# A chain of four convolution layers: how layer 2 takes its first images, gives its last ones to layer 3, and where layer 3's first matrices are loaded

## The chip, the cores and the metric

The kernel runs on one core of a Trainium2 chip. The metric is the device time of one execution in microseconds (us), lower being better; the time of before is the median of three runs. Besides them one execution was profiled, and all starts, waits and durations below are from that one.

## The reference

Four layers, each `x = x + conv_i(groupnorm(x))`, on 32 images of 96 channels and 56 x 56 points, all in fp32 at the edges. `groupnorm` has 32 groups of three channels, so that its mean and variance need every point of three channels of one image.

```python
x = x + _L0_conv_ref(_gn(x), ...)   # 1x1 to 576, 3x3 depthwise, squeeze-excite, 1x1 to 96
x = x + _L1_conv_ref(_gn(x), ...)   # 3-level Haar wavelet, 5x5 depthwise at each level
x = x + _L2_conv_ref(_gn(x), ...)   # 1x1 to 576, 3x3 depthwise, 1x1 to 96, 4-bit quantised
x = x + _L3_conv_ref(_gn(x), L3_conv_diff_metric)   # 9x9 depthwise, kernels from 2x2 metrics
```

## The kernel before

**Layers and intermediates.** Layers 0 and 2 go image by image (channels on partitions); layers 1 and 3 go channel by channel (rows of the image on partitions, all 32 images in the free dimension), layer 1 in 48 pairs of channels. Between the layers x lies in DRAM as `y0`, `y1` and `y2`, each in six tensors of 16 channels (`GR`). In DRAM the 32 images of a point stand side by side, so that one image's piece of a row is 14 floats, 56 B, and that of two images is 112 B. A channel-wise layer can begin only when the last image of the layer before it is stored; an image-wise layer only when the last channel is.

**Who issues transfers, and in which order.** All DMAs are issued by SP, in order, on eight semaphores that I call lanes: a DMA waits until the one eight places before it has landed. In layers 1 and 3 SP's order is written by hand (`MANUAL_SP`, around lines 990 and 1471); in layers 0 and 2 the order of PE, DVE and ACT is (`MANUAL`), and a scheduler puts SP's instructions where it finds them due.

**Layer 1** (lines 785 to 1021). At each step the loads for a pair three ahead are issued; `level1` (939 to 961) makes channel c's result `y` (line 949, three buffers) and stores it to `y1` (958). The matmuls are at lines 892 to 936, the normalisation of x by `nr` is on DVE at 867 and 868. Layer 1's first loads are `X<-y` (735, 738), after the last stores of layer 0, which are left over as `LastStores` (203 to 212) and issued in layer 1.

**From layer 1 to layer 2.** `Layer2` (1024 to 1133) holds two image buffers `pairs`: `kept` (images 0 and 1) and `xt1` (images 2 and 3). While layer 1 runs, `begin` (1117) loads them from `y1` by groups of 16 channels as these are finished, up to group 4. Of the last group, `nearly` (1124) loads 14 channels, 80 to 93, just before channel 94 is finished, in two DMAs of 343 KB; channels 94 and 95 go `straight` (1129) from `y` in SBUF into the buffers, four DMAs of 12 KB each, and also into `y1`. `xt1` first serves as the place where layer 2's weights are quantised. Layer 2 starts with the statistics of image 0 (line 102), then group norms (1202 to 1219) and the quantised activations (1241, 1255), then its first matmuls (1277).

**Layer 2** (1137 to 1376). `add` (1342) finishes a tile of an image, a quarter of its rows; `store` (1354) comes after an image's four. Images are stored by pairs when the second is done (line 225: six DMAs, one a group, 3584 pieces of 112 B). The last two differ: image 30 is stored whole by itself when it is done (six DMAs of 3584 pieces of 56 B); image 31 is stored by tiles as they are finished (`store_tile`, 196, line 200: six DMAs a tile, 896 pieces of 56 B, 49 KB), tiles 0 and 1 in layer 2 and tiles 2 and 3 as `LastStores` in layer 3. Images 30 and 31 both lie in `kept`.

**Layer 3** (1428 to 1507). For each channel: `images` loads X (735, 738, three DMAs), `matrices` loads its banded matrices `raw` (763 to 765: one DMA of 128 partitions, two of 16; 215 KB in all), ACT arranges them as `T` (747), DVE normalises (1460, 1461), 12 matmuls (1468), DVE adds X (1469), and the result is stored (1506). Loads run four channels ahead; every eighth channel the norms of eight channels come in one DMA. The first two left stores are issued between the matrices of channels 0 and 1, two more after channel 1's images, and then one every six channels.

Of the kernel before, what the change touches and what calls it, by code (L numbers as in the profile page):

```python
# [10 lines left out]
F32 = mybir.dt.float32  # L11
# [9 lines left out]
B, C, H, W = 32, 96, 56, 56  # L21
# [10 lines left out]
PH = HH * NPH  # L32
# [3 lines left out]
GR = 16  # L36
# [152 lines left out]
def groups(t, y, at, store=False, of=range(C // GR)):  # L189

    for g in of:
        part = t[g * GR : (g + 1) * GR], at(y[g])
        yield part[::-1] if store else part


def store_tile(nc, y, xt, i, g):

    rows = slice(i * 2 * RT * NPH, (i + 1) * 2 * RT * NPH)
    for to, of in groups(xt[:, rows], y, lambda y: y[:, rows, B - 1, :], store=True, of=[g]):
        nc.sync.dma_start(to, of)  # L200


# [12 lines left out]
def store_images(nc, y, im):  # L215

    b = im["b"]
    if b == B - 2:
        t, at = im["xt"], b
    elif b % 2 and b < B - 1:  # L220
        t, at = im["pair"], slice(b - 1, b + 1)
    else:
        return
    for to, of in groups(t, y, lambda y: y[:, :, at, :], store=True):
        nc.sync.dma_start(to, of)
# [402 lines left out]
NK = 3  # L628
# [128 lines left out]
LOW = 96  # L757


def load_matrices(nc, pool, t, c):  # L760

    raw = pool.tile([128, 2, NK * PH], F32, tag="raw", name="raw")
    nc.sync.dma_start(raw[:, 0], t[c, :128])
    nc.sync.dma_start(raw[LOW:PH, 1], t[c, LOW:PH])
    nc.sync.dma_start(raw[PH:, 1], t[c, 128:])
    return raw
# [18 lines left out]
def layer1(ctx, tc, w, y0, left, made, norm, t1, t2, t3, y1, k2, behind):  # L785
# [4 lines left out]
    nc = tc.nc  # L790
# [148 lines left out]
    def level1(st, j, h):  # L939
        if h == 0:  # L940
            st["y"] = io.tile([PH, 2, B, W4], F32, tag="y", name="y", bufs=3)
        if st["i"]:
            st["pf"][j, h] = pfine.tile([128, W4, B], F32, tag="f", name="pc1")
            coarse(st, j, h, True)
            fine(st, j, h, False)
        else:
            coarse(st, j, h, False)
        ps = st["pf"][j, h]
        nc.vector.scalar_tensor_tensor(
            st["y"][:, h], ps[:PH].rearrange("p q b -> p b q"), st["nr"][j][:PH, 2 * B : 2 * B + 1], st["X"][j][:PH, h],  # L950
            ALU.add, ALU.add)
        if h == 1:
            c = 2 * st["i"] + j
            if c == C - 2:
                k2.nearly()
            if c >= C - 2:
                k2.straight(c, st["y"], 0)
            nc.sync.dma_start(y1[c // GR][c % GR].rearrange("(h p) b q -> p h (b q)", h=2),
                              st["y"].rearrange("p h b q -> p h (b q)"))
            if c >= C - 2:  # L960
                k2.straight(c, st["y"], 1)

    def begin(st):
# [16 lines left out]
    sts = {}  # L980
# [43 lines left out]
class Layer2:  # L1024
# [96 lines left out]
                self.nc.sync.dma_start(pair[g * GR : (g + 1) * GR], self.y1[g][:, :, 2 * i : 2 * i + 2, :])  # L1121
            self.begun = g + 1

    def nearly(self):

        for i, pair in enumerate(self.pairs):
            self.nc.sync.dma_start(pair[C - GR : C - 2], self.y1[-1][: GR - 2, :, 2 * i : 2 * i + 2, :])

    def straight(self, c, y, i):

        for h in range(2):
# [2 lines left out]


@with_exitstack
def layer2(ctx, tc, S, k2, y1, y2):

# [201 lines left out]
    def add(im, i):  # L1342
        for j in range(2):
            n = 2 * i + j
            v = im["xt"][:, 2 * n * 2 * RT : 2 * (n + 1) * 2 * RT, :]
            nc.vector.scalar_tensor_tensor(
                v, im["ps"][i][:C, j, :NT].rearrange("c (r q) -> c r q", q=W4), s3, v, ALU.mult, ALU.add)
        if im["b"] == B - 1:
            tile_stats(nc, parts, im["xt"], i)
            if i < 2:  # L1350
                for g in range(C // GR):
                    store_tile(nc, y2, im["xt"], i, g)

    def store(im):
        b = im["b"]
        if b == B - 1:
            nc.vector.bn_aggr(mv_all[:, B - 1, :], parts.rearrange("c a b -> c (a b)"))
            norm.last(bank(name="pl"))
            return
        channel_stats(nc, sm, im["xt"], mv_all[:, b, :], "t")  # L1360
        store_images(nc, y2, im)
        if b % 2:
            fetch(b + 5)
        if b == B - 2:
            norm.begin()
        del ims[b]
# [6 lines left out]
    with tc.manual_schedule(engines=MANUAL):  # L1373
        others = [t for t in L2_ORDER.split() if t[0] not in "ano" and "+" not in t]
        run_steps(step, image, L2_ORDER, other={-1: L2_FIRST, B - 1: " ".join(others) + L2_LAST, B: "", B + 1: ""})
    return LastStores(nc, y2, k2.pairs[0][:C, :, 1, :], (2, 3)), norm


def diffusion_kernels(tc, cp, w, behind):
# [45 lines left out]


@with_exitstack
def layer3(ctx, tc, w, y2, left, made, norm, td, out):


    nc = tc.nc
    cp = ctx.enter_context(tc.tile_pool(name="l3c", bufs=1, reuse_waits="tile"))
    io = ctx.enter_context(tc.tile_pool(name="l3i", bufs=6, reuse_waits="tile"))
    psum = ctx.enter_context(tc.tile_pool(name="l3p", bufs=8, space=PSUM, reuse_waits="tile"))
    sts = {}

    AHEAD, NN = 4, 8
    norms = {}

    def load_norms(c):  # L1440

        if c % NN == 0:
            norms[c] = io.tile([128, NN, 2 * B + 1], F32, tag="nr", name="nr", bufs=3)
            rows = norm[c : c + NN].rearrange("c x -> (c x)").unsqueeze(0)
            nc.sync.dma_start(norms[c].rearrange("p c x -> p (c x)"), rows.to_broadcast([128, NN * (2 * B + 1)]))

    def matrices(c):
        sts.setdefault(c, {})["raw"] = load_matrices(nc, io, td, c)

    def images(c):  # L1450
        X = sts.setdefault(c, {})["X"] = io.tile([128, 2, B, W4], F32, tag="X", name="X")
        load_halves(nc, X, y2[c // GR][c % GR])

    def normal(st, h):

        if h == 0:
            st["x"] = io.tile([128, 2, B, W4], F32, tag="x", name="x")
        scale, bias = (st["nr"][:, i * B : (i + 1) * B].unsqueeze(2).to_broadcast([128, B, W4]) for i in range(2))
        v = st["x"][:, h]
        nc.vector.tensor_tensor(v, st["X"][:, h], scale, ALU.mult)  # L1460
        nc.vector.tensor_tensor(v, v, bias, ALU.add)  # L1461

    def filtered(st, h):
        if h == 0:
            st["y"] = io.tile([PH, 2, B, W4], F32, tag="y", name="y")
        ps = psum.tile([PH, B, W4], F32, tag="c", name="pc")
        for n, (k, to, of) in enumerate(shifts(W4, NK)):
            nc.tensor.matmul(ps[:, :, to], st["T"][:, h, k, :], st["x"][:, h, :, of], start=(n == 0), stop=(n == NK - 1))  # L1468
        nc.vector.tensor_tensor(st["y"][:, h], ps, st["X"][:PH, h], ALU.add)

    with tc.manual_schedule(engines=MANUAL_SP):
        pick = cp.tile([C, 2, 128], F32, tag="pick", name="pick")
        nc.sync.dma_start(pick, w["pick"])
        matrices(0)
        left.issue(2)
        matrices(1)
        for c in range(2):
            images(c)
        made.store(norm)
        left.issue(2)  # L1480
        images(2)
        load_norms(0)
        matrices(2)
        images(3)
        matrices(3)
        both = cp.tile([128, 2, 2 * B + 1], F32, tag="nr0", name="nr0")
        for c in range(-2, C):
            if 0 <= c < C - AHEAD:
                load_norms(c + AHEAD)
                images(c + AHEAD)  # L1490
                matrices(c + AHEAD)
            if c % 6 == 4:
                left.issue(1)
            cur, far = sts.pop(c, None), sts.get(c + 2)
            if far:
                far["nr"] = norms[(c + 2) // NN * NN][:, (c + 2) % NN] if c >= 0 else both[:, c + 2]
                far["T"] = arranged(nc, io, far["raw"])
                if c == -2:
                    made.spread(both, pick, psum.tile([128, 2, 2 * B + 1], F32, tag="c", name="pr0"))
            for h in range(2):  # L1500
                if far:
                    normal(far, h)
                if cur:
                    filtered(cur, h)
            if cur:
                nc.sync.dma_start(out[c].rearrange("(h p) b q -> p h (b q)", h=2),
                                  cur["y"].rearrange("p h b q -> p h (b q)"))


def kernel_body(tc, w, x, out):  # L1510
    nc = tc.nc
    with ExitStack() as ctx:
# [37 lines left out]
        with ExitStack() as ctx2:  # L1550
            k2 = Layer2(ctx2, tc, S, w, y1, kept, row)

            def behind(pair):
                k2.prepare(pair)
                if not k2.stages:
                    k2.begin(min(2 * pair, C - GR))

            layer1(tc, w, y0, left, made, norm1, t1, t2, t3, y1, k2, behind)
            left, made = layer2(tc, S, k2, y1, y2)
        layer3(tc, w, y2, left, made, norm3, td, out)  # L1560

# [140 lines left out]
```

## Time and profile before

| | |
|---|---|
| runs | 5734.16, 5743.59, 5745.54 us; median 5743.59 |
| the profiled execution | 5735.72 us, of which its span 5733.9 |
| PE, DVE, ACT busy | 96%, 82%, 73% of the span |
| chain of waits, shares | PE 83%, DMA 6%, ACT 4%, DVE 3% |
| last y0 stores land; first matmul of layer 1 | 2667.24; 2674.43 |
| last y of layer 1 (end); first matmul of layer 2 (1277) | 3565.10; 3588.93 |
| last add of layer 2, tile 3 (end); first matmul of layer 3 | 5268.57; 5298.42 |
| layer 3: start of the last matmul | 5728.83 |

Starts are counted from the span's beginning. A lane's landing is the last of a DMA's records. The chain of waits goes back from the last instruction, each step being what released the next; where it lists a DMA, PE and the rest stood waiting for that transfer. The timeline of SP shows when it issued, so a long row of SP is mostly waiting for a lane or for data, not moving bytes.

### The profile page before, as it was taken

What the parts mean: (1) busy time and instruction counts of PE and PEld (TensorE: products, weight loads), DVE (VectorE), ACT (ScalarE), POOL (GpSimd) and SP (SyncE); (2) the same over time, 40 slices, a digit from 0 to 9 for tenths busy, and PEclk for the clock granted to TensorE, in tenths of its full rate; (3) what the DMA queues carried; (4) which work ended last, traced back from release to release, by engine and by line L of the source; (5) the groups of instructions that cost most, each with busy time, mean ns of one, the idle gap of its engine ahead of it and who ended that gap; (6) DMA issues with size and microseconds to landing.
All of it is one profiled execution on the core that took longest, in us unless ns stands there. A gap on an engine that the chain in (4) does not pass through costs nothing.

```text
span 5733.9 us, 137279 instructions
## 1 busy us (share of the span) xinstructions
PE 5498.2 (96%) x59704; PEld 3067.5 (53%) x59704; DVE 4693.9 (82%) x5413; ACT 4173.6 (73%) x6024; POOL 240.2 (4%) x158
## 2 busy tenths in 40 slices
PE   5999999999999999997999998999999999997999
PEld 2333333343333333333566665777788777775444
DVE  6999999999999999996776665767777777774777
ACT  5888888888888888884566554777777777774555
POOL 5000000000000000000000000000000000000000
PEclk9999999999999999997999999999999999998999
DMA  3123333332222332214576667478687796857888
GB/s 99 16 56 61 61 58 58 57 59 48 49 54 56 61 59 53 53 18 73 143 151 148 148 148 111 20 52 48 42 54 44 52 53 41 53 30 46 240 248 247
DMA packets 1306473, 454.45 MB, mean 79 GB/s; under 512 B 1123710, under 2 KB 1301814, under 8 KB 1303950
## 3 DMA queue, kind: packets, MB, share of 16 engines
q1 hardware_dynamic: 1305869, 445.67, 51.5%
q8 instruction: 468, 7.67, 0.6%
q14 instruction: 136, 1.11, 0.1%
HBM read 284.47 MB, written 214.08 MB: 87 GB/s over the span
## 4 chain that ended last, share of the span: by engine, by line
PE 83%; DMA 6%; ACT 4%; DVE 3%; issue 2%; POOL 1%; SPq 1%; ACTq 0%; DVEq 0%; POOLq 0%
PE psd L492 18%; PE psd L1296 13%; PE psj L547 10%; PE ps L425 8%; PE pc L930 7%; PE ps L1277 7%; PE pse L448 6%; PE psj L1339 3%; DMA X<-y 3%; PE pc L1468 2%; PE pc L918 2%; PE pa L892 2%; ACT hi L1247 2%; PE pc L908 1%; ACT u L1267 1%
## 5 line engine op out<-in xcount | busy, mean ns | idle before, releaser
L466 DVE SCALAR_TENSOR_TENSOR h<-hpad,l_wdw,h 128x3136 f32<-128x3136 f32 x512 | 1782.0, 3481 | 9.1
L492 PE MATMUL psd<-plane,filt 128*32 128x392 f32 (+5 forms) x16384 | 1083.3, 485 | 0.0
L1296 PE MATMUL psd<-apad,diag 64*64 64x392 bf16 x20736 | 917.1, 330 | 62.8 <-issue 59.0
L1296 PEld LDWEIGHTS <-diag 64*64 64x64 bf16 x20736 | 689.1, 106 | 285.9 <-issue 111.2
L492 PEld LDWEIGHTS psd<-plane,filt 128*32 128x32 f32 (+1 forms) x16384 | 389.4, 108 | 675.0 <-issue 622.1
L1267 ACT ACTIVATE u<-ps,o,s 128x784 int16<-128x784 f32 x576 | 536.5, 1002 | 164.1 <-PE ps L1277 145.1
L747 ACT COPY T<-raw 32x112 f32<-32x112 f32 (+2 forms) x1440 | 462.9, 384 | 254.8 <-DMA raw<-tdiff 217.4
L1267 ACT ACTIVATE a<-psd,o,s 128x784 int16<-128x784 f32 x448 | 423.7, 998 | 273.3 <-PE psd L1296 273.2
L425 PE MATMUL ps<-xn,l_wboth 96*128 96x392 f32 (+1 forms) x1536 | 465.9, 505 | 23.7 <-ACT xn L407 22.9
L466 DVE SCALAR_TENSOR_TENSOR hc<-hhalf,l_wdw,hc 128x1568 f32<-128x1568 f32 x256 | 473.7, 1850 | 16.2 <-ACT hc L459 9.5
L1277 PE MATMUL ps<-hi,l_w1q 96*128 96x392 f32 x1280 | 463.0, 362 | 6.7 <-DVE u L1265 3.8
L930 PE MATMUL pc<-x,T 128*112 128x416 f32 (+1 forms) x1152 | 446.6, 524 | 3.4 <-DVE x L868 3.4
L1277 PE MATMUL ps<-lo,l_w1q 96*128 96x392 f32 x1280 | 438.2, 342 | 2.9 <-DVE lo L1255 2.9
L1468 PE MATMUL pc<-x,T 128*112 128x416 f32 (+1 forms) x1152 | 420.7, 526 | 18.3 <-DVE x L1461 10.3
L448 PE MATMUL pse<-xn,l_wboth 96*32 96x392 f32 x4096 | 392.3, 501 | 4.5 <-ACT hab L469 4.5
L425 PEld LDWEIGHTS ps<-xn,l_wboth 96*128 96x128 f32 (+1 forms) x1536 | 219.4, 173 | 248.9 <-issue 53.8
L1468 PEld LDWEIGHTS pc<-x,T 128*112 128x112 f32 x1152 | 203.9, 178 | 234.7 <-issue 196.3
L469 ACT ACTIVATE hab<-psd,o,s 128x784 f32<-128x784 f32 x256 | 283.8, 1113 | 59.5 <-PE psd L492 57.5
L435 ACT ACTIVATE hpad<-ps,o,s 128x784 f32<-128x784 f32 x256 | 278.0, 1102 | 50.5 <-PE ps L425 49.0
L547 PE MATMUL psj<-h,wg 128*32 128x392 f32 x3072 | 306.8, 514 | 0.2 <-DVE wg L534 0.2
L547 PE MATMUL psj<-hab,wg 128*32 128x392 f32 x3072 | 305.2, 510 | 0.0
L452 ACT ACTIVATE plane<-pse,o,s 128x784 f32<-128x784 f32 x256 | 255.7, 999 | 26.2 <-PE pse L448 21.6
(265 smaller groups left out, 7622.9 us busy)
## 6 DMA issues: line engine op xcount, KB each, us to landing
X<-y SPq DMA_DIRECT2D x192, 392.0 KB
y<-xt SPq DMA_DIRECT2D x108, 392.0 KB
y<-y SPq DMA_DIRECT2D x96, 392.0 KB
out_dram<-y SPq DMA_DIRECT2D x96, 392.0 KB
twav<-zwav SPq DMA_DIRECT2D x768, 36.8 KB
y<-kept SPq DMA_DIRECT2D x72, 392.0 KB
xt<-y SPq DMA_DIRECT2D x59, 392.0 KB
xt<-in_x_dram SPq DMA_DIRECT2D x8, 2352.0 KB
```

The costliest lines, as they stand in the source:

```text
L425: nc.tensor.matmul(ps[p, j, :NT], wexp[:, k * 128 : k * 128 + 128][:, m], im["xn"][:, j, rows, :].rearrange("c h w -> c (h w)"), start=Tru ...
L448: nc.tensor.matmul(ps[f * GC : (f + 1) * GC, half, :NT].rearrange("p (r w) -> p r w", w=W2), wexp[:, c : c + GC], im["xn"][:, f % 2, r0 : ...
L466: nc.vector.scalar_tensor_tensor(h2, taken(im, k, t), wdw[:, k, t : t + 1], h2, ALU.mult, ALU.add)
L469: nc.scalar.activation(view, ps, AF.Silu, bias=bi[1][:, c : c + 1], scale=sc[1][:, c : c + 1], accum_out=accum)
L492: nc.tensor.matmul(ps[at * GC : (at + 1) * GC, r, :NT].rearrange("p (r w) -> p r w", w=W2)[:, r0 - half * n : r1 - half * n, q0:q1], filt[ ...
L547: nc.tensor.matmul(ps[s * GC : (s + 1) * GC, t, :NT].rearrange("c (m r q) -> c r q m", m=2, q=W4), wg[p, k, c * GC : (c + 1) * GC], phases ...
L747: nc.scalar.copy(to.rearrange("x t (p s) -> x t p s", p=NPH), v[:, k])
L930: nc.tensor.matmul(ps[:PH, to], st["T"][j][:, h, k, :], st["x"][:, j, h, of], start=first and n == 0, stop=not first and n == NK - 1)
L1267: nc.scalar.activation(out, ps, AF.Identity, bias=o[:, c : c + 1], scale=s[:, c : c + 1])
L1277: nc.tensor.matmul(ps[:, j, :NT], w1[:, k * 128 : k * 128 + 128], im[part][:, r0 : r0 + RT, :].rearrange("c h w -> c (h w)"), start=(part ...
L1296: nc.tensor.matmul(ps[q, j, :NT].rearrange("p (r w) -> p r w", w=W), diag[p, k, t, :], v, start=(t == 0), stop=(t == 8))
L1468: nc.tensor.matmul(ps[:, :, to], st["T"][:, h, k, :], st["x"][:, h, :, of], start=(n == 0), stop=(n == NK - 1))
```

## The change

Three parts, which don't depend on each other but share code.

- **Image 30 is stored with image 31.** `store_images` is called only up to image 29. `store_tile` takes both images of `kept`: the same 24 DMAs (12 in layer 2, 12 left for layer 3), each now 896 pieces of 112 B, 98 KB. The six DMAs of image 30 are gone.
- **Matrices of layer 3 are loaded into `xt1`.** When image 28 is finished, `ahead` issues the loads of the matrices of the first nine channels (27 DMAs) into `xt1`, which holds no image by then; nine are as many as fit. Layer 3 uses them in place of its own for c < 9. Layer 3 now runs while layer 2's constants are still allocated.
- **Channels 80 to 95 go straight.** `nearly` is gone; each of the last 16 channels of layer 1 issues two DMAs to `kept`, its store to `y1`, and two DMAs to `xt1`: 64 straight DMAs instead of 8 and the two big loads.

```diff
@@ store_tile
-    for to, of in groups(xt[:, rows], y, lambda y: y[:, rows, B - 1, :], store=True, of=[g]):
+    at = B - 1 if len(xt.shape) == 3 else slice(B - 2, B)
+    for to, of in groups(xt[:, rows], y, lambda y: y[:, rows, at, :], store=True, of=[g]):
@@ load_matrices
-def load_matrices(nc, pool, t, c):
-    raw = pool.tile([128, 2, NK * PH], F32, tag="raw", name="raw")
+def load_matrices(nc, pool, t, c, raw=None):
+    if raw is None:
+        raw = pool.tile([128, 2, NK * PH], F32, tag="raw", name="raw")
@@ layer1, level1
-            if c == C - 2:
-                k2.nearly()
-            if c >= C - 2:
+            if c >= C - GR:
                 k2.straight(c, st["y"], 0)
...
-            if c >= C - 2:
+            if c >= C - GR:
                 k2.straight(c, st["y"], 1)
@@ Layer2
-    def nearly(self):
-        for i, pair in enumerate(self.pairs):
-            self.nc.sync.dma_start(pair[C - GR : C - 2], self.y1[-1][: GR - 2, :, 2 * i : 2 * i + 2, :])
@@ layer2, add
-                    store_tile(nc, y2, im["xt"], i, g)
+                    store_tile(nc, y2, im["pair"], i, g)
@@ layer2, store
-        store_images(nc, y2, im)
+        if b == B - 4:
+            ahead()
+        if b < B - 2:
+            store_images(nc, y2, im)
@@ layer2
-    return LastStores(nc, y2, k2.pairs[0][:C, :, 1, :], (2, 3)), norm
+    return LastStores(nc, y2, k2.pairs[0][:C], (2, 3)), norm
@@ layer3
-        sts.setdefault(c, {})["raw"] = load_matrices(nc, io, td, c)
+        sts.setdefault(c, {})["raw"] = raws[c] if c < len(raws) else load_matrices(nc, io, td, c)
@@ kernel_body
-            left, made = layer2(tc, S, k2, y1, y2)
-        layer3(tc, w, y2, left, made, norm3, td, out)
+            n = 2 * NK * PH
+            room = k2.pairs[1].rearrange("p r i q -> p (r i q)")
+            raws = [room[:, c * n : (c + 1) * n].rearrange("p (a b) -> p a b", a=2) for c in range(room.shape[-1] // n)]
+            def ahead():
+                for c, raw in enumerate(raws):
+                    load_matrices(nc, None, td, c, raw)
+            left, made = layer2(tc, S, k2, y1, y2, ahead)
+            layer3(tc, w, y2, left, made, raws, norm3, td, out)
```

More of the change, by code (lines that the diff above doesn't have):

```diff
@@ L1136, in layer2 @@
 @with_exitstack
-def layer2(ctx, tc, S, k2, y1, y2):
+def layer2(ctx, tc, S, k2, y1, y2, ahead):
     nc = tc.nc
@@ L1427, in layer3 @@
 @with_exitstack
-def layer3(ctx, tc, w, y2, left, made, norm, td, out):
+def layer3(ctx, tc, w, y2, left, made, raws, norm, td, out):
     nc = tc.nc
```

## The prediction

> **What bounds the kernel now.** I read the page first: PE is busy 96% of the span, so time can only be won where PE stands still, or lost where it is made to.
>
> ```profile
> PE 5498.2 (96%) x59704; PEld 3067.5 (53%) x59704; DVE 4693.9 (82%) x5413; ACT 4173.6 (73%) x6024; POOL 240.2 (4%) x158
> ```
>
> The edits touch the seam of layers 0 and 1, layer 1's last eight pairs, the seams of layers 1 and 2 and of layers 2 and 3, and layer 3. The windows of these stretches (columns: stretch, length, busy PE, PEld, DVE, ACT, POOL, granted clock, DMA share, GB/s) show PE nearly empty at two seams, full in layer 1's end and short of full in layer 3:
>
> ```profile
> 3565.00:3589.00 24.00, 0.99 (x5) 0.86 (x5) 5.36 (x18) 1.88 (x2) 2.83 (x15) 0.60 1.36 82
> 3415.00:3565.00 150.00, 149.30 (x576) 90.15 (x576) 89.82 (x134) 75.77 (x204) 0.15 (x1) 1.00 0.61 119
> 5267.00:5299.00 32.00, 2.63 (x10) 2.17 (x10) 5.85 (x18) 5.01 (x15) 0.54 (x1) 0.54 1.01 65
> 5300.00:5733.00 433.00, 419.14 (x1151) 203.12 (x1149) 330.02 (x572) 225.82 (x658) 0.00 (x0) 0.99 0.86 244
> ```
>
> The chain of waits (start, length, what) at the seam of layers 1 and 2: last matmul, y, and then only DMA until layer 2's statistics at line 102.
>
> ```profile
> 3564.41 0.69 DVE y L949
> 3565.10 4.47 SPq L1133
> 3569.62 7.46 DMA kept<-y
> 3577.09 2.64 DMA xt<-y
> ...
> 3579.95 3.85 DVE sth L102 x8
> ```
>
> SP's timeline there says why: two big loads (L1127) stand ahead of the straight copies, and the first straight waits for its turn among eight DMA lanes.
>
> ```profile
> 3558.63 0.88 SPq L1127 DMA_DIRECT2D kept<-y  x1
> 3559.57 3.12 SPq L1127 DMA_DIRECT2D xt<-y  x1
> 3562.73 7.48 SPq L1133 DMA_DIRECT2D kept<-y  x2
> ```
>
> The seam of layers 2 and 3 in the chain, then on SP: the six stores of image 30 hold SP from 5227 to 5256, the twelve tile stores to 5281, and layer 3's first image read (L735) comes only at 5293.
>
> ```profile
> 5276.42 10.68 DMA y<-kept
> 5287.16 5.86 DMA y<-kept
> 5293.44 0.70 SPq L738
> ```
>
> ```profile
> 5227.19 29.21 SPq L225 DMA_DIRECT2D y<-kept  x6
> 5256.50 24.86 SPq L200 DMA_DIRECT2D y<-kept  x12
> ...
> 5285.58 1.90 SPq L200 DMA_DIRECT2D y<-kept  x2
> ...
> 5293.08 0.32 SPq L735 DMA_DIRECT2D X<-y  x1
> ```
>
> **What the Trainium skill says.** "DMA: Bandwidth & Descriptors", Why small descriptors are slow: every packet pays a fixed overhead besides its bytes. The trace agrees: the pair stores (3584 descriptors of 112 B) land 5.9 to 6.9 us apart, mean 6.3, or 1.76 ns a descriptor; image 30's (3584 of 56 B) 5.5 to 8.2, mean 6.8. Half the bytes saved nothing. The same page, Anatomy of one DMA, gives some 2.0 us fixed (written for DMAs issued by GpSimd); SP's smallest straights land 2.1 us or more after issue, so I use 2.1. "TensorE: Matmul & The Clock Gate", What's actually happening: an idle PE falls to half clock. It did at both seams (from 3569.63 to 3607.18 and 5269.47 to 5303.60); both gaps stay long enough to halve it, so I count no gain from the clock.
>
> **Part by part.** *Seam 2/3 (stores).* Removed: six DMAs, 29.2 us of SP and DMA time. Twelve tile stores in layer 2 keep 896 descriptors each, now of 112 B: 1.76 ns x 896 = 1.58 us each, so no dearer. Tile 0's add ends at 5251.17, tile 1's at 5253.17; the twelve begin at 5251.2 on an empty queue and land by about 5251.2 + 12 x 1.58 + latency, 5271.6. Tile 2's add ends at 5266.56, tile 3's at 5268.57: both are over when `pick` (issue 5271.9) and the first two left stores go. The matrix loads that stood between (6 DMAs of 0.4) are gone. Left stores land at about 5275.1, against 5293.03, and the first X read is issued at 5275.15 against 5293.08: **-17.9 us**. The norms' last arithmetic (DVE L153) ended at 5272.84 and channel 0's norms can follow at about 5274.1, so they don't come after X. Bounds: never before tile 3's add plus a store, 5268.6 + 3.5, so at most -21; if the twelve stores took half as long again (9.5 us in all), about -9. That is rival 1.
>
> *Seam 1/2 (straights).* The two big loads (landing 3568.30 and 3575.25) go. After y at 3565.10 four straights, a y store and four straights of the last channel remain, 0.6 us issue each: last issue 3567.95, landing +2.1, 3570.1. Statistics start at 3570.2 instead of 3579.95: **-9.7 us**. Everything behind (norm arithmetic to first matmul at 3588.93, 9.0 us) is unchanged. Bounds -8 to -11.
>
> *Layer 1's end.* 56 small DMAs more, on SP, whose order is written out by hand, ahead of and behind each y store. Per pair of 18.1 us the existing twenty or so DMAs cost SP 8.9 us; eight straights add 4.9 (0.6 each), 13.8 of 18.1. Queued behind them are the loads of later pairs (x, matrices, norms); DVE's line 867 waits for norms and PE for DVE. In before, SP was clogged 20 us at 3448 by the group-4 loads of 343 KB; DVE then waited 3.3 us for norms, and PE lost 0.7 us of 165. The clog now takes longer to work off, and y has three buffers, each held until its straights land. Taken **+1 us**, bounds 0 to +5; I exclude a gain, as PE is full there.
>
> *Layer 3's matrices.* Nine channels' 27 loads leave layer 3: 27 x 0.43 = 11.6 us of SP issue, 9 x 215 KB = 1.9 MB, 7.9 us at the measured 244 GB/s. The 128-partition ones go where SP is idle (5112 to 5173, between pair stores): nothing. In layer 3, PE loses 433.00 - 419.14 = 13.9 us, of which 12.3 are stalls over 0.6 us, all at channels 15 to 63 where norms and left stores are put in between; out stores lag 2.6 to 5 us behind y all along. A head start of 8 to 12 us of SP and DMA time is partly eaten, because prefetch depth is limited by six X buffers and DMA is at 86% anyway. I take a third of the stalls: **-4 us**, bounds 0 and -12 (all stalls).
>
> *Seam 0/1 (moved loads).* The order of SP's instructions in the changed kernel shows what the diff doesn't: the eighteen 16-partition loads, whose rows no image uses, are put by the scheduler into layer 1. Four stand between the last four y0 stores (landed 2667.24) and the first X read, and the first waits for the norms' arithmetic (DVE L153, ended 2669.80).
>
> ```profile
> 2656.49 7.40 SPq L200 DMA_DIRECT2D y<-kept  x4
> 2667.39 0.30 SPq L735 DMA_DIRECT2D X<-y  x1
> ```
>
> Then X is issued at 2669.85 + 4 x 0.45 = 2671.7, 4.3 us later; X had 1.7 us to spare behind the norms' copy (ACT L163, 2672.40) so **+2.7 us**, bounds 0 to +4.5. The other fourteen lie one to three a time among pairs with over 5 us of idle SP: nothing, or 0.5 us each if that cover were gone.
>
> *Sum:* -17.9 - 9.7 + 1 - 4 + 2.7 = -27.9. The profiled execution took 5735.7 (span 5733.9), giving 5707.8; the median of the three runs is 5743.6, 7.9 above it, so I forecast 5743.6 - 27.9 = **5716**. Bounds combined as independent: about 8 us.
>
> **Rivals.** *1. Seam 2/3 gives half* (-9): the 112 B tile stores queue behind pair stores or cost more when read while DVE writes beside them. For: 24 stores carry twice the bytes. Against: 1.76 ns a descriptor at 112 B. 5743.6 - 27.9 + 8.9 = 5725.
> *2. Layer 3's stalls all go:* -12.3 instead of -4. For: the lag is a fixed backlog, and a head start stays if nothing refills it. Against: DMA at 0.86. 5743.6 - 36.2 = 5707.
> *3. It doesn't do what it says:* the preload starts in layer 1, not in an idle stretch; its start costs 4.5 and layer 3 keeps its stalls: 5743.6 - 22.1 = 5722.
> *4. Slower: the straights starve layer 1's end.* The break-even is (18.1 - 8.9)/8 = 1.15 us of SP per straight. In before the eight took 7.48 + 1.24 + 1.24 + 1.95 = 11.9 us, 1.5 each with lane waits. If each waited for the landing of one before it, 2.1 us: 8.9 + 16.8 = 25.7 a pair, 7.6 over, eight pairs 61, less 7 of slack: +54 in place of +1, so 5743.6 - 27.9 + 53 = 5769. Against: 3.4 of those 11.9 belong to the big loads, lanes were otherwise free (seven DMAs in a row issued 0.45 apart), and the last three pairs have no loads left to delay.
>
> **Chances.** Forecast 0.57; rival 1 0.15; rival 2 0.13; rival 3 0.09; rival 4 0.06. Range 5698 to 5735: below, rival 2 with the run-to-run spread of some 9 us; above, rival 1 with layer 1's bounds. About 0.2%, 11.5 us, is what a measurement of this kernel can tell from no change: faster means under 5732, which all cases but rival 4 and the tail of rival 1 give: 0.90, 0.05, 0.05.
>
> **What would show it.** Statistics at about 9.7 us earlier against the last y (15 us before, about 5 after); first layer-3 X issue 6.6 us after tile 3's add instead of 24.5; first matmul of layer 1 2.7 us later after its last y0 store; stalls of layer 3 at the same channels, about 8 us in all; PE's busy time in layer 1's last 150 us still over 148. The forecast is wrong if PE shows holes in that stretch, or if image reads of layer 3 wait for something other than left stores.

## The result, and the profile after

The changed kernel took 5713.89 us (median of four runs, 5709.17 to 5716.10) against 5744.57 for the kernel before in the same comparison: a ratio of 0.9946, 95% interval 0.9929 to 0.9964. The forecast was 5716, range 5698 to 5735. The profiled execution took 5714.57, its span 5712.6, 21.3 less than that of before.

The first line of the page shows PE's work unchanged in number. PE was busy 3.8 us less than before; the other 17.5 us of the shorter span are time in which it no longer stood still.

```profile
PE 5494.4 (96%) x59704; PEld 3068.1 (54%) x59704; DVE 4692.3 (82%) x5413; ACT 4174.0 (73%) x6024; POOL 240.6 (4%) x158
```

Since PE runs the same 59704 matmuls in the same order in both, the n-th start of one trace can be set beside the n-th of the other. The difference after less before, stretch by stretch. "Layer 1's last 13 pairs" are its last 910 matmuls; the eight pairs of the prediction are among them and hold all of the difference. Layer 2 begins here with its first matmul of the group norms (3584.35 in before), not with line 1277, and ends with the norms' first matmul after its last image:

| stretch | before | after | difference | forecast |
|---|---|---|---|---|
| first matmul of the program to first of layer 1 | 2655.9 | 2657.4 | +1.6 | +2.7 |
| of it, norms' arithmetic (L153) to that matmul | 4.63 | 7.14 | +2.5 | +2.7 |
| layer 1's last 13 pairs | 235.0 | 236.3 | +1.3 | +1 |
| last matmul of layer 1 to first of layer 2 | 20.5 | 10.7 | -9.8 | -9.7 |
| layer 2, first to last matmul | 1685.9 | 1689.7 | +3.8 | 0 |
| tile 3's add to first matmul of layer 3 | 29.9 | 14.1 | -15.7 | -17.9 |
| layer 3, first to last matmul | 430.4 | 428.2 | -2.2 | -4 |

The windows of after over three of the stretches shown of before, moved with the work (+2.65, +2.65 and -3.3 us): layer 1's end lost PE 1.3 us more, and at the two seams PE now works 7 of 24 and 18 of 32 us, where it worked 1 and 2.6, since the next layer begins inside the window. (The columns are as in the prediction.)

```profile
3417.65:3567.65 150.00, 148.05 (x570) 89.40 (x568) 89.20 (x133) 75.09 (x201) 0.15 (x1) 1.00 0.60 123
3567.65:3591.65 24.00, 7.27 (x20) 5.53 (x20) 15.08 (x37) 9.06 (x7) 2.83 (x15) 0.58 1.48 75
5263.70:5295.70 32.00, 18.04 (x45) 9.25 (x46) 14.72 (x32) 17.08 (x51) 0.54 (x1) 0.73 0.56 118
```

Seam of layers 1 and 2, VectorE's timeline of after (the bracket is the idle time before, and what ended it): statistics start 5.03 us after the last y, where it was 14.86.

```profile
3567.06 0.68 DVE L951 SCALAR_TENSOR_TENSOR y<-pc,nr,X 112x448 f32<-112x448 f32 x1 [1.68 <-PE pc L932]
3572.78 3.84 DVE L102 BATCH_NORM_STATS2 sth<-kept 96x6 f32<-96x392 f32 x8 [5.03 <-DMA xt<-y]
```

SP's timeline there: the straight copies stand alone, and issue as soon as y is there. The two of channel 95's `xt` landed at 3572.30 and 3572.46.

```profile
3568.33 0.58 SPq L958 DMA_DIRECT2D y<-y  x1
3568.97 1.27 SPq L1128 DMA_DIRECT2D xt<-y  x2
```

Seam of layers 2 and 3, SP's timeline of after: the long row of image 30's stores is gone, the queue stands empty from the last pair store, the twelve tile stores start with tile 0's add (5247.81), and X is issued at 5274.32, 9.1 us after tile 3's add (5265.22); before it was 24.5 after.

```profile
5194.81 6.50 SPq L226 DMA_DIRECT2D y<-xt  x1
5247.83 16.13 SPq L201 DMA_DIRECT2D y<-kept  x12
5264.06 1.33 SPq L1471 DMA_DIRECT2D pick<-in_pick_dram  x1
5265.48 1.81 SPq L201 DMA_DIRECT2D y<-kept  x2
5274.32 0.30 SPq L736 DMA_DIRECT2D X<-y  x1
```

Seam of layers 0 and 1, SP's timeline of after: four preloads (xt<-tdiff) before the first X, the first of them at 2668.70, just after the norms' arithmetic ended at 2668.64, though the y0 stores had landed at 2666.01.

```profile
2655.32 7.42 SPq L201 DMA_DIRECT2D y<-kept  x4
2668.70 0.31 SPq L766 DMA_DIRECT2D xt<-tdiff  x1
2669.07 0.41 SPq L767 DMA_DIRECT2D xt<-tdiff  x1
2669.53 0.41 SPq L766 DMA_DIRECT2D xt<-tdiff  x1
2669.99 0.42 SPq L767 DMA_DIRECT2D xt<-tdiff  x1
2670.57 0.32 SPq L736 DMA_DIRECT2D X<-y  x1
```

### The profile page after: what moved, and what is told of

It is laid out like the page before. It is cut to its first block, busy times and chain, and to the rows that moved or that the text cites. A ratio compares the mean times of both kernels' runs of the same rounds, so it can differ in the third digit from the quotient of the medians.

```text
span 5712.6 us, 137352 instructions
## 1 busy us (share of the span) xinstructions
PE 5494.4 (96%) x59704; PEld 3068.1 (54%) x59704; DVE 4692.3 (82%) x5413; ACT 4174.0 (73%) x6024; POOL 240.6 (4%) x158
## 4 chain that ended last, share of the span: by engine, by line
PE 81%; DMA 6%; ACT 4%; DVE 4%; issue 2%; SPq 1%; POOL 1%; ACTq 0%; DVEq 0%; POOLq 0%
PE psd L493 17%; PE psd L1291 13%; PE psj L548 10%; PE ps L426 7%; PE pc L932 7%; PE ps L1272 6%; PE pse L449 6%; PE psj L1334 3%; DMA X<-y 3%; PE pc L920 2%; ACT hi L1242 2%; PE pa L894 2%; PE pc L1466 2%; PE pc L910 1%; DMA raw<-tdiff 1%
## 5 line engine op out<-in xcount | busy, mean ns | idle before, releaser
L748 ACT COPY T<-raw 128x112 f32<-128x112 f32 (+2 forms) x1386 | 445.6, 385 | 221.9 <-DMA raw<-tdiff 164.1
L1466 PE MATMUL pc<-x,T 128*112 128x416 f32 (+1 forms) x1152 | 419.4, 525 | 15.0 <-DVE x L1459 10.5
L453 ACT ACTIVATE plane<-pse,o,s 128x784 f32<-128x784 f32 x256 | 255.9, 1000 | 25.0 <-PE pse L449 20.3
```

The lines of the kernel that those rows point to most:

```text
L748: nc.scalar.copy(to.rearrange("x t (p s) -> x t p s", p=NPH), v[:, k])
```

## The experiments

My theory was the sum of the prediction with the stretches above in place of the forecasts, and layer 2's +3.8 as chance. The rivals gave layer 2's loss, layer 3's small gain or the size of the seam to one edit or another. Two tables hold what was measured; the paragraphs say what follows. The columns of the first are, in us: norms' arithmetic to layer 1's first matmul; layer 1's last 13 pairs; last matmul of layer 1 to first of layer 2; tile 3's add to layer 3's first matmul; layer 3; layer 2 (from the second matmul of line 1277 to the norms' first one at its end).

| kernel | start | 13 pairs | seam 1/2 | seam 2/3 | layer 3 | layer 2 |
|---|---|---|---|---|---|---|
| before | 4.63 | 235.0 | 20.5 | 29.9 | 430.4 | 1678.6 |
| e7, before again | 4.63 | 235.0 | 20.3 | 19.4 | 431.4 | 1693.4 |
| e1, stores alone | 4.64 | 234.9 | 20.5 | 10.6 | 437.4 | 1693.6 |
| e12, stores, left ones single | 4.64 | 235.0 | 20.1 | 13.9 | 429.2 | 1695.4 |
| e2, straights alone | 4.63 | 234.9 | 10.5 | 23.4 | 428.8 | 1678.0 |
| e3, preload alone | 7.10 | 235.0 | 20.7 | 24.1 | 422.7 | 1699.1 |
| after | 7.14 | 236.3 | 10.7 | 14.1 | 428.2 | 1682.4 |
| e8, after again | 7.32 | 235.9 | 10.6 | 10.5 | 428.0 | 1676.8 |
| e10, after again | 7.40 | 235.6 | 10.8 | 10.5 | 426.9 | 1677.5 |
| e4, preload held back | 4.63 | 236.0 | 10.5 | 10.2 | 426.5 | 1693.6 |
| e5, half of image 30 early (tiles 2, 3) | 7.30 | 235.8 | 10.6 | 10.3 | 423.9 | 1680.0 |
| e6, half of image 30 early (tiles 0, 1) | 7.65 | 237.9 | 10.6 | 9.6 | 427.4 | 1695.9 |
| e11, e6 again | 7.17 | 237.9 | 10.8 | 9.6 | 424.1 | 1675.9 |
| e9, e5 and e4 together | 4.64 | 236.4 | 10.5 | 10.3 | 422.7 | 1679.6 |

Times, as ratios to the kernel before run beside them:

| kernel | median us (runs) | ratio | 95% interval |
|---|---|---|---|
| e1 | 5730.5 (14) | 0.9986 | 0.9977 to 0.9996 |
| e2 | 5728.1 (22) | 0.9981 | 0.9972 to 0.9990 |
| e3 | 5739.6 (13) | 1.0001 | 0.9988 to 1.0014 |
| e4 | 5718.7 (5) | 0.9966 | 0.9954 to 0.9978 |
| e5 | 5702.5 (4) | 0.9928 | 0.9913 to 0.9943 |
| e6 | 5719.3 (4) | 0.9959 | 0.9944 to 0.9974 |
| e8 | 5707.4 (4) | 0.9937 | 0.9920 to 0.9953 |
| e9 | 5704.9 (6) | 0.9940 | 0.9923 to 0.9958 |
| e10 | 5714.7 (6) | 0.9950 | 0.9932 to 0.9968 |
| e11 | 5704.7 (6) | 0.9937 | 0.9921 to 0.9953 |
| e12 | 5733.8 (10) | 0.9974 | 0.9962 to 0.9987 |

### The three parts, each alone

**e1: the stores.** Edit, on before:

```diff
-    for to, of in groups(xt[:, rows], y, lambda y: y[:, rows, B - 1, :], store=True, of=[g]):
+    at = B - 1 if len(xt.shape) == 3 else slice(B - 2, B)
+    for to, of in groups(xt[:, rows], y, lambda y: y[:, rows, at, :], store=True, of=[g]):
...
-                    store_tile(nc, y2, im["xt"], i, g)
+                    store_tile(nc, y2, im["pair"], i, g)
...
-        store_images(nc, y2, im)
+        if b < B - 2:
+            store_images(nc, y2, im)
...
-    return LastStores(nc, y2, k2.pairs[0][:C, :, 1, :], (2, 3)), norm
+    return LastStores(nc, y2, k2.pairs[0][:C], (2, 3)), norm
```

> Image 30's stores joined with image 31's, nothing else changed. Theory (the terms add up and belong to the edits they were put down to): first matmul of layer 3 comes about 14 us earlier against the end of tile 3's add (29.9 us before), since the six matrix DMAs still stand before X; layer 3 itself as before; -14, so about 5731. Rival (the seam's gain is mostly that of the missing matrix loads): 8 or less, 5737. Rival (the 3.8 us that layer 2 lost between the two traces belong to the joined stores): layer 2 is 3 to 4 us longer here, and the whole gives -10.

The seam was 10.6 us, 9 to 19 less than in the four traces with image 30 stored by itself (19.4, 23.4, 24.1, 29.9), although the matrix loads still stood there; the rival of the missing loads falls. But layer 3 took 437.4, 7 more than before: that I had not expected. Of the seam's 13.6 us (24.2 on average in those four) it leaves some 6, and the medians differ by 6.3 (0.14%).

**e2: the straights.**

```diff
-            if c == C - 2:
-                k2.nearly()
-            if c >= C - 2:
+            if c >= C - GR:
                 k2.straight(c, st["y"], 0)
...
-            if c >= C - 2:
+            if c >= C - GR:
                 k2.straight(c, st["y"], 1)
```

> Channels 80 to 95 straight, nothing else changed. Theory: the statistics start 5.0 us after the last y instead of 14.9 (-9.8), layer 1's last eight pairs cost +1.3, layer 2 unchanged; -8.5, about 5736. Rival (layer 2's loss of 3.8 belongs to the earlier start, its image loads coming no sooner): PE's lead of 7 to 8 us is 4 us smaller by the end of layer 2; -5, about 5740.

Seam 10.5 against 20.5: all of the gain is this part's. Layer 1's end cost nothing here, where I expected 1.3; layer 2 lost nothing. The median fell 8.7 us, where 8.5 were expected.

**e3: the preload**, that is the change without the two edits above.

> The first nine channels' matrices preloaded, nothing else changed. Theory: +2.6 at layer 1's start for the four small loads that stand before the first X, -1 to -2 at the seam of layers 2 and 3 for the six DMAs gone, -2 in layer 3; -1, about 5743, which is no difference. Rival (layer 3's stalls go with the loads): -6 or more, 5738.

Start 7.10 against 4.63, as expected. Layer 3 took 422.7, 6 to 9 less than in the four traces that have neither preload nor joined left stores (428.8 to 431.4), where I expected 2: the rival was right on layer 3. The seam stayed at 24.1, so the six matrix loads gone from it saved nothing that shows. The waits of PE in layer 3 (engine, line, what it waited for: total us, times, longest) show where it came from. Before, in its second trace:

```profile
PE pc L1468 <- ACT T L747: 9.8, 15, 1.9
PE pc L1468 <- DVE x L1461: 9.6, 3, 7.7
```

And with the preload alone:

```profile
PE pc L1471 <- DVE x L1464: 5.8, 3, 5.4
PE pc L1471 <- ACT T L747: 4.0, 6, 1.3
```

The longest wait for x (7.7 and 5.4) ends with the layer's first matmul, so it belongs to the seam. The many short ones are for the arranged matrices T. T alone varies from trace to trace (8.0, 4.7 and 6.2 in before's first, e2 and e12), so I go by all the time that PE stood inside layer 3: 9.2 to 11.9 us in the four traces without preload or joined left stores, 4.9 here. By its stretches this kernel should have been some 5 us quicker than before; its median was no different, with an interval of 7 us either way. Layer 2 was the longest of all in its trace, 1699.1.

### What layer 3 gave back

**e5: tiles 2 and 3 of image 30 early.** Edit, on after:

```diff
+        if b == B - 2:
+            rows = slice(4 * RT * NPH, None)
+            for to, of in groups(im["xt"][:, rows], y2, lambda y: y[:, rows, b, :], store=True):
+                nc.sync.dma_start(to, of)
-    return LastStores(nc, y2, k2.pairs[0][:C], (2, 3)), norm
+    return LastStores(nc, y2, k2.pairs[0][:C, :, 1, :], (2, 3)), norm
```

> The whole change, but tiles 2 and 3 of image 30 are stored by themselves when image 30 is done (six DMAs of 1792 pieces of 56 B, in the 38 us in which SP and the queues are empty), so that the twelve left stores carry image 31 alone, 56 B a piece. Theory (the left stores' doubled bytes are what gave layer 3 back its head start): layer 3 takes 422 to 424 us from first to last matmul, as with the preload alone (422.7), against 428.2 and 426.5 with the joined stores; seam of layers 2 and 3 unchanged at 10 to 14 us from the last add to the first matmul; about 5 us below the change. Rival (layer 3 is longer because it starts earlier, with less fetched): 426 to 428 stays.

Layer 3 took 423.9, the seam 10.3; inside layer 3 PE stood 6.5 us, against 8.6 in the changed kernel's trace beside it (e8). The median was 5.0 below the changed kernel's (5702.46 against 5707.44), as expected, but the two intervals overlap, so that the times alone don't show it. SP's timeline shows the six added stores in the empty stretch, over before the tile stores begin:

```profile
5167.83 32.98 SPq L226 DMA_DIRECT2D y<-xt  x6
5222.26 11.22 SPq L1363 DMA_DIRECT2D y<-kept  x6
5244.76 13.61 SPq L201 DMA_DIRECT2D y<-kept  x12
```

**e12: the same on the stores alone.** Edit: e1 with the lines of e5.

> The stores' part alone, as in the first experiment, but with tiles 2 and 3 of image 30 stored by themselves when it is done, so that only the twelve tile stores of layer 2 are joined and the twelve left stores are of 56 B pieces. Theory (layer 3's extra time lies in the left stores' doubled bytes): layer 3 429 to 431 us from first to last matmul, as in the kernel before (428.8 to 431.4), against 437.4 with joined left stores, and the seam stays near 10.6 us. Rival (layer 3 is longer because the seam is shorter, so that less is fetched ahead): about 437 again.

Layer 3 took 429.2, as expected; the seam was 13.9, 3.3 longer than in e1, so the rival (short seam, long layer 3) is not quite excluded by this run alone. e5 and e9 speak against it: there the seam was as short as in e1, and layer 3 shorter than in every trace with joined left stores. PE's waits in layer 3, with joined left stores (e1):

```profile
PE pc L1470 <- ACT T L748: 14.5, 16, 2.0
PE pc L1470 <- DVE x L1463: 6.1, 3, 5.3
```

and with single ones (e12):

```profile
PE pc L1474 <- DVE x L1467: 10.5, 7, 7.5
PE pc L1474 <- ACT T L748: 6.2, 8, 1.3
```

The waits for T go from 14.5 to 6.2, and all that PE stood inside layer 3 from 15.5 to 9.6. The two kernels ran on different chips; but on each chip where both kinds were traced, the single ones had the shorter layer 3: e2's 428.8 against e1's 437.4; e5's 423.9 against 428.0 and 427.4 (e8, e6); e9's 422.7 against 426.9 and 424.1 (e10, e11).

The X read behind each of the last eight left stores took, from issue to landing, 6.0 to 6.2 us on average in the seven traces with joined ones, and 5.2 to 5.7 in the seven with single ones (means 6.1 and 5.5). So a joined left store delays the read behind it by some 0.6 us; at 244 GB/s its 49 KB more would be 0.2. Eight times 0.6 is 5 us, of the size of what layer 3 lost (8 here, about 4 with the preload), but the delay is not passed on to PE one for one: e11's reads took 6.2 us, and its layer 3 only 424.1. Why a left store of 112 B pieces costs more is open; that the read behind it is later is shown.

**e6: tiles 0 and 1 early instead**, the left stores staying joined.

```diff
-                    store_tile(nc, y2, im["pair"], i, g)
+                    store_tile(nc, y2, im["xt"], i, g)
...
+        if b == B - 2:
+            rows = slice(0, 4 * RT * NPH)
+            for to, of in groups(im["xt"][:, rows], y2, lambda y: y[:, rows, b, :], store=True):
+                nc.sync.dma_start(to, of)
```

> The whole change, but tiles 0 and 1 of image 30 are stored by themselves when image 30 is done, so that the twelve tile stores in layer 2 carry image 31 alone at 56 B a piece; the left stores stay joined. Theory (cost by descriptor): a tile store lands every 1.5 us or so as it did in two of the three traces of joined stores, so the seam stays within 2 us of 10 to 14 and layer 3 at 426 to 428; no difference from the change. Rival (112 B tile stores are dearer, 1.95 us as in the trace of the change): the seam shortens by up to 4 us.

Seam 9.6, layer 3 427.4: the theory's side. Tile stores of 56 B landed 1.57 us apart, joined ones 1.95, 1.59, 1.62 and 1.54 in the four traces of after and e4, so the 1.95 of the first trace was chance. Layer 1's end was 237.9, some 2 us longer than in the changed kernel, here and when the program ran again (e11), though the edit isn't there; why is open. All four runs were 8.7 us or more above the slowest of the changed kernel's beside them (5708.6), more than that explains.

### The moved loads

**e4: the preload held back until image 28.**

```diff
             def ahead():
+                nc.vector.memset(room[LOW:, : len(raws) * n : NK * PH], 0.0)
```

> The whole change, with all 27 preloads held back until image 28 by one small write on VectorE (18 elements a partition) that they follow, so that none stands in layer 1. Theory: layer 1's first matmul comes 2.6 us sooner after the last y0 store, and nothing else moves; 5714 - 2.6 = 5711. Rival (the first X was late for another reason, and the small loads are free): 5714, with the first matmul where it is.

Start 4.63: the 2.5 us are the four small loads'. In the median they can't be seen (0.9966). e4 ran on the same chip as e1, e2 and e3, and the parts add up there: the three ratios together give -0.32%, this kernel -0.34%. SP's timeline at the seam of layers 0 and 1 with the loads held back, from e9, has X where it was in before:

```profile
2656.78 7.37 SPq L201 DMA_DIRECT2D y<-kept  x4
2667.46 0.30 SPq L736 DMA_DIRECT2D X<-y  x1
```

### Layer 2's wander

**e7: before again; e8 and e10: after again; e11: e6 again.** None has an edit of its own.

> The kernel before, unchanged, for a second trace. Theory (its first trace was slow at the seam and quick in layer 2, both by chance): last add to first matmul of layer 3 23 to 26 us instead of 29.9, layer 2 from first to last matmul 1680 to 1700 instead of 1678.6, layer 3 429 to 431. Rival (the differences between the traces belong to the edits): 29 to 30 and 1677 to 1680.

> The changed kernel, unchanged, for a second trace and more times. Theory: last add to first matmul 10 to 14 us, layer 3 426 to 429, layer 2 anywhere from 1678 to 1700, layer 1's first matmul 7.1 us after the norms' arithmetic, layer 1's last eight pairs 236 us; the whole 5710 to 5720.

> The changed kernel, unchanged, a third time, for times beside the kernel before. Theory (the edited stretches are worth 21 to 26 us, and the rest of the difference between the medians is layer 2's own wander, which differs from one loading of a program to the next): the ratio can come out anywhere from 0.993 to 0.998, the stretches as before within 2 us. Rival (the change shortens layer 2 by something the traces do not name): 0.993 to 0.995 again, layer 2 at 1676 to 1683.

> Tiles 0 and 1 of image 30 stored by themselves, again, since all four of its runs were some 12 us above the change on the same chip although every edited stretch was as short. Theory (layer 2's wander goes with a loading of the program): now it is within 5 us of the change, with layer 2 away from its 1696. Rival (it goes with the program): some 12 us above again, layer 2 at 1694 to 1698.

Before's second trace had the seam at 19.4, shorter than the 23 to 26 that I expected, in the main because image 30's six stores landed 6.0 us apart there and 6.8 in the first; the tile stores behind them came closer too (1.3 us apart, 1.5 in the first). SP's timeline of e7:

```profile
5240.47 26.23 SPq L225 DMA_DIRECT2D y<-kept  x6
5266.80 21.11 SPq L200 DMA_DIRECT2D y<-kept  x12
...
5297.72 0.32 SPq L735 DMA_DIRECT2D X<-y  x1
```

The same program, run as e6 and as e11, had layer 2 at 1695.9 and at 1675.9, and medians of 5719.3 and 5704.7, 11.9 above and 10.0 below the changed kernel beside it (I had expected within 5 for the second). So layer 2 wanders by 20 us without any edit. PE's waits in layer 2 (3600 to 5240), for e6:

```profile
PE psd L1291 <- issue: 68.9, 72, 3.1
```

and for e11:

```profile
PE psd L1291 <- issue: 57.0, 68, 2.2
```

The depthwise matmuls of line 1291 stand waiting for nothing that the profile names ("issue"), and longer in the one than in the other. A part can be seen: over the first 45 us of layer 2 the granted clock (0.59 and 0.75; it is the figure before the last two) came back later in e6, and about 5 of the 20 us are lost there.

```profile
3581.00:3626.00 45.00, 34.52 (x234) 30.55 (x235) 30.66 (x61) 29.28 (x27) 1.15 (x2) 0.59 1.26 46
3579.00:3624.00 45.00, 34.05 (x362) 29.13 (x364) 30.90 (x61) 31.74 (x30) 1.15 (x2) 0.75 1.26 46
```

Why the clock came back later, and what lengthens the rest, is open. e8's layer 2, 1676.8, and its median, 5707.4, were both below what I expected. e10's rival, a change that shortens layer 2, is not excluded by e8 and e10 alone (1676.8, 1677.5), but e4 (1693.6) and e6 (1695.9), with the same layer 2, speak against it.

### Both mends

**e9: e5 with e4's line.**

> The change with both mends: tiles 2 and 3 of image 30 stored by themselves when image 30 is done, and all 27 preloads held back until image 28. Theory: layer 1's first matmul 4.6 us after the norms' arithmetic (7.1 to 7.3 in the change), layer 3 422 to 424 us; 5 + 2.5 us below the change on the same chip. Rival (the two mends meet in one queue: 27 preloads and the six stores come one after the other near image 28 and 30): layer 2's end or the seam becomes 3 us longer and eats the second half.

Start 4.64, seam 10.3, layer 3 422.7: as expected; the rival's 3 us at the seam did not come. Layer 1's end kept its loss (236.4). Beside it the changed kernel (e10) took 5714.7, 9.7 more; the two intervals overlap, and layer 2's wander is larger than the expected 7.5.

## Why the prediction was right, point by point

- **Seam 1/2, -9.7:** measured -9.8 in the first pair of traces and again with this part alone. The chain was rightly read: DMA and lanes only, and nothing late behind it.
- **Seam 0/1, +2.7:** +2.5 to 2.8, and gone when the loads are held back. Only the order of instructions showed this one; the diff doesn't. So far rival 3 was right, and it was in the sum.
- **Layer 1's end, +1:** 0.6 to 1.3 in the traces of after, nearly all of it in one stall of PE (at 3484 in after's time), after the group-4 loads as said; VectorE's wait for norms there grew from 3.3 to 4.8 us. With the straights alone it was 0, in the same order on SP: the X read behind the group-4 loads held SP 6.5 us there, 7.1 to 7.5 in after, e4 and e6. So the straights alone don't make the stall; why that read waited longer is open. Rival 4, the slower one, lacked its hold: a straight cost SP 0.5 to 0.8 us, not 1.15.
- **Seam 2/3, -17.9:** mis-sized. The first pair gave -15.7; over the traces, image 30 by itself took (29.9 + 19.4 + 23.4 + 24.1)/4 = 24.2 and the changed kernel with e4 (14.1 + 10.5 + 10.5 + 10.2)/4 = 11.3, so -12.9. The store of 1.58 us and X at 6.6 us after tile 3's add were near (5.2 to 5.6 in three traces, 9.1 in the first). The failing number was the 29.9 of before: one execution, in which the 56 B stores were slow, taken for the kernel's own. Rival 1's half had -9; the truth lay between.
- **Layer 3, -4:** the net was near (-2.2 in the first pair; the changed kernel with e4 427.4 on average against 429.9 for the four without preload or joined left stores, so -2.5), and the working was wrong three times. The 13.9 us that PE was said to lose count 3.7 after the last matmul's end (5729.35, in a window that runs to 5733): inside the layer PE stood 10.2, so that 12.3 of stalls can't be a part of it. The preload alone is worth some -7, more than a third of the stalls (rival 2 had all; 4.9 us were left). And a term was missing: ten of the left stores land in layer 3, and the change doubles their bytes. I wrote "so no dearer" for the twelve in layer 2 and carried it to the left ones without costing them beside X reads; alone they cost 7 to 8 us (one trace), with the preload about 4 (424.1 to 428.2 against 422.7 to 423.9).
- **The sum, -27.9:** by the corrected stretches it is +2.7 + 1.0 - 9.8 - 12.9 - 2.5 = -21.5. The medians fell by 31, 37 and 25 us in three comparisons, each with an interval of some 10 either way. The missing 3 to 15 us aren't in any edited stretch; layer 2's wander of 20 us, which differs between two runs of one program, is large enough for them. For the second comparison it shows: the traced runs e7 and e8 lie 36.4 us apart, as far as the medians, and layer 2 is 16.6 of it (1693.4 and 1676.8). For the others it can't be shown: in the first, the traced pair lies 21.2 apart and layer 2 was longer after. In e4's comparison the miss is the other way: its stretches make 24 us, the medians differ by 18. So the nearness of 5714 to 5716 is in part luck: two terms were too large, and something outside the edited stretches, layer 2 where it can be seen, made up for them.

## What to carry to other kernels

Set the n-th instruction of one trace beside the n-th of the other before explaining a total: it tells at once which stretch changed, and which wanders in every run. Take the "before" of a stretch from more than one execution where it hangs on stores, since one of them may be 10 us off. When stores are made fatter to save their number, cost them at every place where they are issued: with nothing but stores queued they cost little, between reads that feed the next matmuls each delayed the read behind it by some 0.6 us, and the layer was 4 to 8 us longer.

## What the runs showed of the hardware that I had not expected

When only stores were queued, those of 896 pieces landed nearly as fast with twice the bytes: every 1.3 to 1.6 us with pieces of 56 B (before 1.52, e7 1.31, e2 1.34, e3 1.43, e6 1.57, e11 1.52), every 1.5 to 1.6 with 112 B in six traces (e8 1.59), 1.75 in e12 and 1.95 in the first trace of after. The means are 1.45 and 1.64, so the doubling cost 0.2 us, not nothing as the prediction had it. That agrees with the Trainium skill, "DMA: Bandwidth & Descriptors", Why small descriptors are slow, in so far as most of the cost goes with the number. But the same doubling, put between X reads, made the read behind each store land 0.6 us later (6.1 against 5.5, seven traces each), which that rule doesn't give.
